# Three DRAM accumulators instead of four in a graph layer's scatter-add

## The chip, the cores and the metric

The kernel runs on one core of one Trainium2 chip. The metric is the device time of one execution in microseconds (us), as the median of several runs.

## The reference

One layer of a graph network with 6250 nodes, 200,000 edges and 128 features. Node rows are normalised and multiplied by a matrix; each edge makes a filter from its 20 attributes, multiplies it into the row of its `dst` node, and the products are added up at its `src` node; two small layers and a residual follow. Cut to what matters:

```python
h = jnp.maximum(_layernorm(x), 0.0)
xw = h @ W_in
W_ij = (shifted_softplus(f_ij @ W_f1 + b_f1) @ W_f2 + b_f2) * f_ij_cutoff
x_ij = xw[dst] * W_ij
out = jax.ops.segment_sum(x_ij, src, num_segments=6250)
return x + shifted_softplus(out @ W_o1 + b_o1) @ W_o2 + b_o2
```

`dst` is sorted and `src` is random, so reading node rows is local and adding the products up is not.

## The kernel before

**Quads.** 512 edges make a quad; there are 391 of them, in four chunks of 128 edges each (the last has fewer). The main loop runs over quads as a software pipeline: in iteration i, stage 1 of quad i (the filter's first layer: `s1_pe`, `s1_exp`, `s1_ln`), stage 2 of quad i-1 (filter and node rows on PE, `s2_copy` on ACT, and `s2_m`, the product, on DVE), then stage 3 of older quads. Everything else hangs in the iterations as hooks, under points such as "L" (loads), "D0", "PE2" or "S", which `run(i, point)` calls in a fixed order. So the order on each engine is written out by hand.

**Three ways to sum.** 168 quads are *sorted*: their rows are permuted by one-hot products and added up on PE into `accT`, a tile in SBUF that holds the sum with features on the partitions; what does not fit goes out in one overflow scatter for two quads (84 in all). The other 223 quads are *plain*: each chunk's 128 rows are added into DRAM by `scatter` (line 594), an indirect accumulating DMA issued by GpSimd (POOL). Of the plain quads 31 combine rows with equal `src` within the chunk first; 192 are *listed*, in 12 windows of 16: repeated rows go to list rows behind the accumulator, and at a window's end `l_load` reads these rows of every accumulator, `l_sum` adds them up by one matrix product per accumulator, and one further scatter adds the result. In all there are 768 + 123 + 96 = 987 scatters.

**Accumulators in DRAM.** There are `NACC` copies `accs[k]` (6272 node rows, 128 rows for rejects, and the list rows). `acc_of` deals the scatters out by their number n; two that add to the same copy may not overlap, so a scatter waits until the last one on its copy has landed. Before:

```python
        if k < K2_END:
            return k % 2
        if k < K3_END:
            return k % 3
        if k < RET:
            return k % 4
        return 1 + k % 3
```

`K2_END` is 8, `K3_END` 140, and `RET` is the number of scatters less 64, that is 923. The copies come into use one after the other because each must be filled with zeros first: `zero_piece` writes a copy's node rows in ten transfers, copies 0 and 1 from GpSimd's queue, copies 2 and 3 from SyncE's (SP) in the iterations of `Z2` and `Z3`; `zero_list` writes the list rows in three transfers.

**Retiring a copy.** After scatter 923 nothing is added to copy 0. From a few iterations later its rows are read in 13 groups of up to 512 nodes (`r0_load`, SP), transposed on PE (`r0_tp`) and added into `accT` on DVE (`r0_add`, line 1097), one group per iteration that has room.

**Output stage.** After the loop comes a check whose `For_i` blocks redo the work where an edge fell outside the fixed windows (on these inputs they run zero times). The output stage then loads three copies per group (`t_load`), adds them (`t_sum1` on GpSimd, `t_sum2` on GpSimd and DVE in turn), transposes, adds `accT`, and applies the two layers and the residual. Loads run five groups ahead (`TAIL_AHEAD`).

**Queues.** SP issues nearly all loads in program order, POOL issues the scatters in program order. DVE writes the product rows `s` of a listed quad, which the scatter reads, into a ring of four buffers.

Of the kernel before, what the change touches and what calls it, by code (L numbers as in the profile page):

```python
# [7 lines left out]
F32 = mybir.dt.float32  # L8
# [5 lines left out]
ALU = mybir.AluOpType  # L14
# [6 lines left out]
P = 128  # L21
# [22 lines left out]
WSEG = 256  # L44
HB = 64
NR = 3 * WIN
NACC = 4
FPARTS = ((0, 3), (3, 2), (5, 1))
CQ = 16
EARLY_N = 256  # L50
# [4 lines left out]
def tile_gnn(ctx: ExitStack, tc: tile.TileContext, x, fB, cT, srcT, srcr, dstr, win_, wf1, wf2, bias, bo1c, wo1,  # L55
             wo2, consts, ident, cmap, out, n_edges):
    nc = tc.nc
# [9 lines left out]
    spread = big(NSC)  # L67
    NCH = -(-n_edges // P)
    NQ = -(-NCH // 4)
    NPT = NP // P  # L70
    groups = node_groups(NP)
    tgroups = [(g * 512, min(4, (NP - g * 512) // P)) for g in range(-(-NP // 512))]
# [3 lines left out]
    GN = NP // GRP  # L76
    ZR = 10 if ACC_R % 10 == 0 else 1
    ZL = 3
    K1_END, K2_END, K3_END = 2, 8, 140
    Z2, Z3 = [0,0,1,1,2,2,3,3,4,4], [5+2*j for j in range(10)]  # L80
    mpq = sorted_quads(NQ)
    mpi = {q: n for n, q in enumerate(mpq)}
    units = unit_its(mpq)
    splain = [q for q in range(NQ) if q not in mpi]
    plain = {q: n for n, q in enumerate(splain)}
    NS = len(splain)
    LB, LE = listed(NS) if spread else (0, 0)
    CE = min(128, EP // P) if spread else EP // P
    CB = min(4 * NS + 64, EP // P) if spread else 0
    lend = splain[LE - 1] if LE else 0  # L90
    scat = [0] * (NQ + 60)
    for q in splain:
        scat[q + (2 if LB <= plain[q] < LE else 4)] += min(4, NCH - 4 * q)
    NW = (LE - LB) // SW
    LR = P * NW
    wend = [splain[LB + SW * (w + 1) - 1] for w in range(NW)]
    for w in range(NW):
        scat[wend[w] + 16] += 1
    for q in mpq[1::2] + mpq[-1:] * (len(mpq) % 2):
        scat[q + 10] += 1  # L100
    RET = max(120, sum(scat) - 64)
    ret_at = min(i for i in range(len(scat)) if sum(scat[:i + 1]) >= RET)

    cp = ctx.enter_context(tc.tile_pool(name="cp", bufs=1))
    dp = ctx.enter_context(tc.tile_pool(name="dp", bufs=1, space=DRAM))
# [1 line left out]
    ld = edge.enter_context(tc.tile_pool(name="ld", bufs=3))  # L107
    wk = edge.enter_context(tc.tile_pool(name="wk", bufs=2))
    sp_ = edge.enter_context(tc.tile_pool(name="sp", bufs=4))
    ps = edge.enter_context(tc.tile_pool(name="ps", bufs=2, space=PSUM))  # L110

    accs = []
# [15 lines left out]
    idt = cp.tile([P, P], F32, name="idt")  # L128
# [11 lines left out]
    accT = cp.tile([P, NP], F32, name="accT")  # L140
# [33 lines left out]

    def rows(t, o, T):
        n = min(T, 2)
        return t[o:o + T * P, :].rearrange("(h p t) f -> p h (t f)", p=P, t=n)

    def wide(t, T):
        return t.rearrange("p (h t) f -> p h (t f)", t=min(T, 2))  # L180

    def nodes(t, o, T):
        return t[:, o:o + T * P].rearrange("f (h p t) -> f h t p", p=P, t=min(T, 2))

    def tiles(t, T):
        return t[:, :T].rearrange("f (h t) p -> f h t p", t=min(T, 2))
# [5 lines left out]
    pst = {}  # L192
# [388 lines left out]
    def acc_of(k):  # L581
        if k < K1_END:
            return 0
        if k < K2_END:
            return k % 2
        if k < K3_END:
            return k % 3
        if k < RET:
            return k % 4
        return 1 + k % 3  # L590

    sc_n = [0]

# [256 lines left out]
    with tc.manual_schedule():  # L850
# [113 lines left out]
        def at(i, point, fn, *a):  # L964
            hooks.setdefault((i, point), []).append((fn, a))
# [6 lines left out]
        if CE < EP // P:  # L972
            w = (CE + 4 * NS) // 2
# [22 lines left out]
            at(2 * k + 3 if spread else 0, "D2", half_piece, k)  # L996
        for j in range(ZR):
            at(Z2[j] if spread else 0, "L", zero_piece, nc.sync, 2, j)
        for j in range(ZR):
            at(Z3[j] if spread else 0, "L", zero_piece, nc.sync, 3, j)  # L1000
        for g in range(1, NG):
            if not spread:
                xt_load(g)
# [74 lines left out]
        def large_all():  # L1078
            nc.vector.tensor_scalar(zcol[:, 3:4], late["lps"][:, 0:1], 0.0, None, op0=ALU.is_gt)

        def r0_load(g):
            o, T = tgroups[g]
            t_ = ld.tile([P, 4, P], F32, tag="fb", name="r0t", bufs=2)
            nc.sync.dma_start(wide(t_[:, :T], T), rows(accs[0], o, T))
            pst["r", g] = t_

        def r0_tp(g):
            T = tgroups[g][1]
            tp = ps.tile([P, 4, P], F32, tag="B", name="rtp", bufs=4)
            for t in range(T):  # L1090
                nc.tensor.transpose(tp[:, t, :], pst["r", g][:, t, :], idt)
            pst["p", g] = tp

        def r0_add(g):
            o, T = tgroups[g]
            v = nodes(accT, o, T)
            nc.vector.tensor_tensor(v, tiles(pst["p", g], T), v, op=ALU.add)

        def x_bias(t):
            n = min(4, NPT - t)  # L1100
            v = x_sb[:, t:t + n]
# [20 lines left out]
        for t in range(0, NPT, 4):  # L1122
            i = mid + 8 * (t // 4) if spread else 0
            at(min(i + 9, NQ + 1), "D2", x_bias, t)
        r0_at = 0
        for g in range(len(tgroups)):
            i = clear(max(r0_at + 1, ret_at + 5), units)
            r0_at = i
            at(i - 2, "L", r0_load, g)
            at(i, "PE2", r0_tp, g)  # L1130
            at(i + 1, "D0", r0_add, g)
        for r in range(-(-len(mpq) // RKQ)):
            i = mpq[RKQ * r]
            i = max(i, 6)
# [44 lines left out]
        if LE:  # L1179
            for k in range(NACC):  # L1180
                for j in range(ZL):
                    at((0, 3, 6, 9)[k] + j + 1, "L", zero_list, k, j)
        for q in mpq:
            at(q + 1, "D2", perm_oh, q)
            at(q + 2, "DR", part_rem, q, 1)
# [27 lines left out]
        for r in range(len(mpq) // RND):  # L1213
            for s, k in enumerate(unit_slots(mpq, r)):
# [2 lines left out]
                at(k, "PE2", unit_pe, r, s)  # L1217
                at(k + 1, "D1", unit_evac, r, s)

        banked = (prep_tp, prep_mm, rank_count, rank_over, permute, over_pe, over_row, over_sum, late_bias, r0_tp,  # L1220
                  l_count, l_sum, l_before, l_place)
        full = {-1: False}
        r0_end = r0_at
        s1_pe(0)
        for i in range(max(NQ + 7, last + 16, r0_end + 2, lend + 24)):
            if i % 2 == 0 and i // 2 + 2 <= (NQ - 1) // 2:
                load_sc(i // 2 + 2)
            run(i, "L")
            run(i, "D0")
            if i < NQ:  # L1230
                s1_oh(i)
            run(i, "D1")
            if 0 <= i - 1 < NQ:
                s1_eq(i - 1)
            if 0 <= i - 1 < NQ:
                s2_pe_x(i - 1)
                s2_pe_w(i - 1)
            if i + 1 < NQ:
                s1_pe(i + 1)
            if i < NQ:  # L1240
                s1_exp(i)
                s1_ln(i)
            if 0 <= i - 3 < NQ and not full[i - 1]:
                s3_copy(i - 3, 0)
                s3_copy(i - 3, 1)
            run(i, "A0")
            if 0 <= i - 4 < NQ:
                s3_ji(i - 4)
            run(i, "A1")
            if 0 <= i - 1 < NQ:  # L1250
                s2_copy(i - 1)
            run(i, "DM")
            if 0 <= i - 1 < NQ:
                s2_m(i - 1)
            if 0 <= i - 3 < NQ:
                s3_idx(i - 3)
            run(i, "DR")
            run(i, "PE1")
            full[i] = sum(fn in banked for fn, _ in hooks.get((i, "PE2"), [])) > 2
            if 0 <= i - 2 < NQ:  # L1260
                s3_pe(i - 2)
                if full[i]:
                    s3_copy(i - 2, 0)
                    s3_copy(i - 2, 1)
            run(i, "PE2")
            run(i, "A2")
            run(i, "D2")
            if 0 <= i - 4 < NQ and plainq(i - 4):
                s3_scatter(i - 4)
            if 0 <= i - 2 < NQ and i - 2 not in mpi and not plainq(i - 2):  # L1270
                s3_scatter(i - 2)
            run(i, "S")
# [20 lines left out]
    with tc.For_i(0, redo, 1):  # L1293
        anew = nc.values_load(flagi[:, 1:2], min_val=0, max_val=1, skip_runtime_bounds_check_because="0 or 1")
        with tc.For_i(0, anew, 1):
            nc.vector.memset(accT, 0.0)
            for k in range(1, NACC):
                for j in range(ZR):
                    zero_piece(nc.sync, k, j)
        trips = nc.values_load(flagi[:, 0:1], min_val=0, max_val=NCH,  # L1300
# [70 lines left out]
    with tc.manual_schedule():  # L1371
# [8 lines left out]

        def t_sum1(g):
            T = tgroups[g][1]
            a2 = tl[g][2]
            nc.gpsimd.tensor_tensor(a2[:, :T], a2[:, :T], tl[g][3][:, :T], op=ALU.add)

        def t_sum2(g):
            T = tgroups[g][1]
            a1 = tl[g][1]
            eng = nc.vector if g % 2 else nc.gpsimd
            eng.tensor_tensor(a1[:, :T], a1[:, :T], tl[g][2][:, :T], op=ALU.add)  # L1390

        def t_tp(g):
            tp = pt.tile([P, 4, P], F32, tag="tp", name="tp")
            for t in range(tgroups[g][1]):
                nc.tensor.transpose(tp[:, t, :], tl[g][1][:, t, :], idt)
            tl[g]["tp"] = tp

        def t_cp(g):
# [52 lines left out]
            del tl[g]  # L1451

        for g in range(min(TAIL_AHEAD, TG)):
            for k in (1, 2, 3):
                t_load(g, k)
        for j in range(-1, TG + 4):
            if TAIL_AHEAD <= j + TAIL_AHEAD < TG:
                for k in (1, 2, 3):
                    t_load(j + TAIL_AHEAD, k)
            if j + 1 < TG:  # L1460
                t_sum1(j + 1)
                t_sum2(j + 1)
            if 0 <= j < TG:
                t_tp(j)
            if 0 <= j - 1 < TG:
                t_cp(j - 1)
                t_z(j - 1)
            if 0 <= j - 3 < TG:
                t_act(j - 3)
                t_y(j - 3)  # L1470
            if 0 <= j - 1 < TG:
                t_ln(j - 1)
            if 0 <= j - 4 < TG:
                t_out(j - 4)
# [32 lines left out]
def clear(i, busy, n=1):  # L1507
    while any(i + k in busy for k in range(n)):
        i += 1
    return i  # L1510
# [113 lines left out]
```

## Time and profile before

| what | value |
|---|---|
| runs, median (lowest to highest) | 2063.21 us (2060.39 to 2073.85) |
| profiled execution, time / span | 2063.64 us / 2061.9 us |
| PE, DVE, ACT, POOL busy | 1820.4, 1650.9, 1470.8, 1652.4 us |
| scatters on POOL | 987, first at 57.8 us, last at 2007.3 us |
| output stage | about 2009 us to the end of the span |
| DMA | 272.41 MB, mean 132 GB/s |
| mean granted clock of PE | 0.952 |

Busy time is the time in which an engine executes; register, branch and DMA-issuing instructions of SP are not counted. A scatter counts as busy on POOL while its descriptors are made, not until its rows have landed. "Idle before, releaser" is the time in which an engine stood still ahead of an instruction, and what ended that; "issue" means that nothing that the profile shows was waited for. A row `line engine op out<-in xcount` groups like instructions, with their minimum, median and maximum time in ns in a view of one line. PE is TensorE, DVE VectorE, ACT ScalarE.

### The profile page before, as it was taken

What the parts mean: (1) busy time and instruction counts of PE and PEld (TensorE: products, weight loads), DVE (VectorE), ACT (ScalarE), POOL (GpSimd) and SP (SyncE); (2) the same over time, 40 slices, a digit from 0 to 9 for tenths busy, and PEclk for the clock granted to TensorE, in tenths of its full rate; (3) what the DMA queues carried; (4) which work ended last, traced back from release to release, by engine and by line L of the source; (5) the groups of instructions that cost most, each with busy time, mean ns of one, the idle gap of its engine ahead of it and who ended that gap; (6) DMA issues with size and microseconds to landing.
All of it is one profiled execution on the core that took longest, in us unless ns stands there. A gap on an engine that the chain in (4) does not pass through costs nothing.

```text
span 2061.9 us, 54889 instructions
## 1 busy us (share of the span) xinstructions
PE 1820.4 (88%) x19121; PEld 1188.1 (58%) x19121; DVE 1650.9 (80%) x4449; ACT 1470.8 (71%) x3999; POOL 1652.4 (80%) x1040
## 2 busy tenths in 40 slices
PE   2578998899999999899989999999799899999966
PEld 1455555556655665565656566566565556666734
DVE  3577897798987988888888989888788687787745
ACT  2458776777777787777778787787677677788714
POOL 3578887888888888878788888888888888888884
PEclk9789999999999999999999999999999999999987
DMA  6887766667676776667666666766666666667647
GB/s 240 242 202 141 129 123 123 111 111 144 118 136 120 128 136 111 130 115 131 129 121 125 121 126 117 126 117 132 113 116 114 125 105 118 108 119 141 128 44 250
DMA packets 359675, 272.41 MB, mean 132 GB/s; under 512 B 97727, under 2 KB 319850, under 8 KB 359394
## 3 DMA queue, kind: packets, MB, share of 16 engines
q0 software_dynamic: 143728, 71.30, 34.4%
q1 hardware_dynamic: 215378, 197.50, 32.8%
q8 instruction: 151, 2.47, 0.5%
q14 instruction: 130, 1.06, 0.2%
q10 hardware_dynamic: 288, 0.07, 0.0%
HBM read 154.45 MB, written 114.24 MB: 130 GB/s over the span
## 4 chain that ended last, share of the span: by engine, by line
PE 46%; DVE 20%; ACT 10%; DMA 7%; issue 6%; POOL 5%; SPq 4%; DVEq 0%; ACTq 0%; POOLq 0%
PE pq L702 15%; PE W L520 10%; PE un L795 8%; POOL acc L597 5%; ACT xc L525 3%; PE po L715 2%; DVE accT L806 2%; DVE pt L691 2%; PE z L328 2%; ACT mst L708 2%; DVE eql L384 2%; PE xg L512 2%; DMA acc<-s,lji 2%; DVE pm L677 2%; ACT a L333 2%
## 5 line engine op out<-in xcount | busy, mean ns | idle before, releaser
L597 POOL DMA_INDIRECT acc<-s,lji x768 | 1254.4, 1633 | 250.4 <-issue 185.5
L702 PE MATMUL pq<-pt,pm 128*128 128x387 bf16 x2688 | 545.6, 346 | 43.2 <-ACT pt L697 10.6
L525 ACT ACTIVATE xc<-xg,cb 128x128 f32<-128x128 f32 x1564 | 448.0, 377 | 80.5 <-PE xg L512 73.4
L520 PE MATMUL W<-w,a 128*128 128x128 f32 x3128 | 467.7, 294 | 0.0
L520 PEld LDWEIGHTS W<-w,a 128*128 128x128 f32 x3128 | 392.2, 197 | 42.9 <-issue 4.5
L708 ACT CAST mst<-pq 128x387 bf16<-128x387 f32 x672 | 305.4, 481 | 149.7 <-PE pq L702 108.7
L702 PEld LDWEIGHTS <-pm 128*128 128x128 bf16 x2688 | 261.1, 100 | 235.6 <-issue 60.9
L795 PE MATMUL un<-so,mst 32*128 32x392 bf16 x8064 | 372.5, 327 | 11.9 <-ACT s L555 5.8
L795 PEld LDWEIGHTS <-mst 32*128 32x128 bf16 x8064 | 226.1, 93 | 152.0 <-issue 45.3
L338 ACT ACTIVATE a<-a,con 128x512 f32<-128x512 f32 x391 | 282.3, 722 | 12.7
L597 POOL DMA_INDIRECT acc<-s,ji x123 | 198.4, 1613 | 80.1 <-issue 26.7
L333 ACT ACTIVATE a<-z 128x512 f32<-128x512 f32 x391 | 238.0, 609 | 30.5 <-PE z L328 20.1
L691 DVE TENSOR_TENSOR pt<-pt 128x512 f32<-128x512 f32 x336 | 231.6, 689 | 5.8
L535 DVE TENSOR_TENSOR pt<-W,xc 128x512 f32<-128x512 f32 x168 | 115.5, 687 | 132.4 <-PE po L715 62.9
L677 DVE TENSOR_SCALAR pm<-iot,pos 128x576 bf16<-128x576 f16 x672 | 219.8, 388 | 0.0
L535 DVE TENSOR_TENSOR s<-W,xc 128x512 f32<-128x512 f32 x192 | 131.8, 686 | 75.7 <-ACT xc L525 44.6
L780 DVE TENSOR_SCALAR so<-iot,mst 128x392 bf16<-128x392 f16 x672 | 181.2, 333 | 9.7 <-PE un L795 9.2
L597 POOL DMA_INDIRECT acc<-os,oji x96 | 158.1, 1647 | 30.4 <-issue 18.3
L806 DVE TENSOR_TENSOR accT<-un,accT 128x392 f32<-128x392 f32 x320 | 158.4, 557 | 28.6 <-PE un L795 18.9
L512 PE MATMUL xg<-wn,oh 63*128 63x128 bf16 x1564 | 158.9, 224 | 25.0 <-DVE oh L345 13.8
L328 PE MATMUL z<-ft,ws 123*128 123x512 bf16 x391 | 151.7, 388 | 15.5 <-POOL b2rep L942 9.3
L509 PE MATMUL W<-b2rep,onesb 64*128 64x512 bf16 x391 | 155.6, 398 | 0.2 <-issue 0.2
(210 smaller groups left out, 1968.1 us busy)
## 6 DMA issues: line engine op xcount, KB each, us to landing
rb<-reld SPq DMA_DIRECT2D x391, 64.0 KB
fsd<-f SPq DMA_DIRECT2D x49, 480.0 KB
ft<-fsd SPq DMA_DIRECT2D x195, 120.0 KB
sb<-src SPq DMA_DIRECT2D x169, 128.0 KB
fb<-in_fB_dram SPq DMA_DIRECT2D x49, 320.0 KB
ft<-fsd SPq DMA_DIRECT2D x195, 80.0 KB
wn<-tab SPq DMA_DIRECT2D x782, 15.8 KB
acc<-s,lji POOLq DMA_INDIRECT x768
```

Source lines behind the costliest of these rows:

```text
L333: nc.scalar.activation(a, st[q]["z"], AF.Exp)
L338: nc.scalar.activation(a, a, AF.Ln, bias=half, scale=0.5)
L512: nc.tensor.matmul(xg[:, c, :], st[q]["oh"][a:a + NR, c * P:(c + 1) * P], wn[a:a + NR, c // 2, :], start=True, stop=True)
L520: nc.tensor.matmul(W[:, c, :], st[q]["a"][:, c * P:(c + 1) * P], w2, start=False, stop=(c == 3))
L525: nc.scalar.mul(xc[:, c, :], st[q]["xg"][:, c, :], late["c", q // CQ][:, 4 * (q % CQ) + c:4 * (q % CQ) + c + 1])
L535: nc.vector.tensor_tensor(m[:, :, :P], st[q]["W"], st[q]["xc"], op=ALU.mult)
L597: nc.gpsimd.indirect_dma_start(out=accs[k][:rows, :], out_offset=bass.IndirectOffsetOnAxis(ap=ji, axis=0), in_=s, in_offset=None, compute_ ...
L677: nc.vector.tensor_scalar(pm[:, c], iot[:, :SLOTS], rk[r]["pos"][:, 4 * j + c:4 * j + c + 1], None, op0=ALU.is_equal)
L691: nc.vector.tensor_tensor(pt[:, :, k * P:(k + 1) * P], a, high(a), op=ALU.subtract)
L702: nc.tensor.matmul(t[:, :PW], mp[q]["pm"][:, c, s * P:(s + 1) * P], high(mp[q]["pt"][:, c:c + 1, :PW])[:, 0], start=(c == 0), stop=(c == 3))
L708: nc.scalar.copy(mp[q]["ms", s][:, :PW], mp[q].pop(("q", s))[:, :PW])
L795: nc.tensor.matmul(ts[g][:, :GN], mp[q]["ms", s][v, k * P:(k + 1) * P], mp[q]["oh"][v], start=(q == qs[0] and k == 0), stop=(q == qs[-1] a ...
```

## The change

There are three copies in DRAM. From scatter 8 on they take turns by three up to the end. The fourth copy's fills are gone (ten transfers and three list transfers), each window reads and adds three lists instead of four, copy 0 is no longer read and added into `accT` on the way, and the output stage reads copies 0, 1 and 2 instead of 1, 2 and 3.

```diff
-NACC = 4
+NACC = 3
...
-    K1_END, K2_END, K3_END = 2, 8, 140
-    Z2, Z3 = [0,0,1,1,2,2,3,3,4,4], [5+2*j for j in range(10)]
+    K1_END, K2_END = 2, 8
+    Z2 = [0, 0, 1, 1, 2, 2, 3, 3, 4, 4]
...
         if k < K2_END:
             return k % 2
-        if k < K3_END:
-            return k % 3
-        if k < RET:
-            return k % 4
-        return 1 + k % 3
+        return k % 3
...
-        for j in range(ZR):
-            at(Z3[j] if spread else 0, "L", zero_piece, nc.sync, 3, j)
...
-        def r0_load(g):
-            o, T = tgroups[g]
-            t_ = ld.tile([P, 4, P], F32, tag="fb", name="r0t", bufs=2)
-            nc.sync.dma_start(wide(t_[:, :T], T), rows(accs[0], o, T))
-            pst["r", g] = t_
-
-        def r0_tp(g):
-            T = tgroups[g][1]
-            tp = ps.tile([P, 4, P], F32, tag="B", name="rtp", bufs=4)
-            for t in range(T):
-                nc.tensor.transpose(tp[:, t, :], pst["r", g][:, t, :], idt)
-            pst["p", g] = tp
-
-        def r0_add(g):
-            o, T = tgroups[g]
-            v = nodes(accT, o, T)
-            nc.vector.tensor_tensor(v, tiles(pst["p", g], T), v, op=ALU.add)
...
-        r0_at = 0
-        for g in range(len(tgroups)):
-            i = clear(max(r0_at + 1, ret_at + 5), units)
-            r0_at = i
-            at(i - 2, "L", r0_load, g)
-            at(i, "PE2", r0_tp, g)
-            at(i + 1, "D0", r0_add, g)
...
-                    at((0, 3, 6, 9)[k] + j + 1, "L", zero_list, k, j)
+                    at((0, 3, 6)[k] + j + 1, "L", zero_list, k, j)
...
-            for k in range(1, NACC):
+            for k in range(NACC):
                 for j in range(ZR):
                     zero_piece(nc.sync, k, j)
...
         for g in range(min(TAIL_AHEAD, TG)):
-            for k in (1, 2, 3):
+            for k in range(NACC):
                 t_load(g, k)
```

In the output stage `t_sum1`, `t_sum2` and `t_tp` use the tiles of copies 0, 1 and 2 accordingly. The reckoning of `RET` (`scat`, `ret_at`) is removed, as is `r0_tp` from the list of functions that use PSUM's "B" banks, by which the loop decides where the evacuations of a combined quad stand on ACT.

More of the change, by code (lines that the diff above doesn't have):

```diff
@@ L90, in tile_gnn @@
     lend = splain[LE - 1] if LE else 0
-    scat = [0] * (NQ + 60)
-    for q in splain:
-        scat[q + (2 if LB <= plain[q] < LE else 4)] += min(4, NCH - 4 * q)
     NW = (LE - LB) // SW
@@ L96, in tile_gnn @@
     wend = [splain[LB + SW * (w + 1) - 1] for w in range(NW)]
[L97 to L102, printed above, removed]
     cp = ctx.enter_context(tc.tile_pool(name="cp", bufs=1))
@@ L1218, in tile_gnn @@
                 at(k + 1, "D1", unit_evac, r, s)
-        banked = (prep_tp, prep_mm, rank_count, rank_over, permute, over_pe, over_row, over_sum, late_bias, r0_tp,
+        banked = (prep_tp, prep_mm, rank_count, rank_over, permute, over_pe, over_row, over_sum, late_bias,
                   l_count, l_sum, l_before, l_place)
         full = {-1: False}
-        r0_end = r0_at
         s1_pe(0)
-        for i in range(max(NQ + 7, last + 16, r0_end + 2, lend + 24)):
+        for i in range(max(NQ + 7, last + 16, lend + 24)):
             if i % 2 == 0 and i // 2 + 2 <= (NQ - 1) // 2:
@@ L1382, in t_sum1 @@
             T = tgroups[g][1]
-            a2 = tl[g][2]
-            nc.gpsimd.tensor_tensor(a2[:, :T], a2[:, :T], tl[g][3][:, :T], op=ALU.add)
+            a1 = tl[g][1]
+            nc.gpsimd.tensor_tensor(a1[:, :T], a1[:, :T], tl[g][2][:, :T], op=ALU.add)
         def t_sum2(g):
             T = tgroups[g][1]
-            a1 = tl[g][1]
+            a0 = tl[g][0]
             eng = nc.vector if g % 2 else nc.gpsimd
-            eng.tensor_tensor(a1[:, :T], a1[:, :T], tl[g][2][:, :T], op=ALU.add)
+            eng.tensor_tensor(a0[:, :T], a0[:, :T], tl[g][1][:, :T], op=ALU.add)
         def t_tp(g):
@@ L1394, in t_tp @@
             for t in range(tgroups[g][1]):
-                nc.tensor.transpose(tp[:, t, :], tl[g][1][:, t, :], idt)
+                nc.tensor.transpose(tp[:, t, :], tl[g][0][:, t, :], idt)
             tl[g]["tp"] = tp
@@ L1457, in tile_gnn @@
             if TAIL_AHEAD <= j + TAIL_AHEAD < TG:
-                for k in (1, 2, 3):
+                for k in range(NACC):
                     t_load(j + TAIL_AHEAD, k)
```

## The prediction

> **What bounds the kernel now.** I read the page first (busy times, costliest groups), then busy time by stage, then what GpSimd waited for in each stage, and last the timeline around single scatters.
>
> ```profile
> span 2061.9 us, 54889 instructions
> PE 1820.4 (88%) x19121; PEld 1188.1 (58%) x19121; DVE 1650.9 (80%) x4449; ACT 1470.8 (71%) x3999; POOL 1652.4 (80%) x1040
> PE 46%; DVE 20%; ACT 10%; DMA 7%; issue 6%; POOL 5%; SPq 4%; DVEq 0%; ACTq 0%; POOLq 0%
> L597 POOL DMA_INDIRECT acc<-s,lji x768 | 1254.4, 1633 | 250.4 <-issue 185.5
> ```
>
> By these rows PE is the busiest and fills most of the chain that ended last, while POOL, 80% busy, has 5% of it. But a POOL instruction is always followed by a gap, and the gap is no spare time. From the stage 1090 to 1887 us:
>
> ```profile
>   issue: 98.2, 322
>   DMA acc<-s,lji: 6.7, 22
> ```
>
> 322 gaps in which nothing was waited for make 98.2 us, 0.305 us each; the 22 put down to a landing are the same length (6.7 by 22), so no landing delayed anything there. With 0.305 us for each scatter added to POOL's busy time, the stages read differently:
>
> ```profile
> core 0: us, PE busy (x) PEld busy (x) DVE busy (x) ACT busy (x) POOL busy (x), PEclk, DMA share, GB/s
> 173.00:357.00 184.00, 165.02 (x1675) 105.29 (x1676) 147.71 (x411) 133.08 (x367) 150.30 (x92) 0.94 0.67 125
> 357.00:840.00 483.00, 448.63 (x4882) 289.29 (x4880) 418.77 (x1163) 369.06 (x1014) 406.05 (x250) 0.98 0.68 125
> 840.00:1090.00 250.00, 226.71 (x2426) 145.72 (x2424) 212.58 (x605) 182.38 (x501) 202.67 (x124) 0.97 0.66 122
> 1090.00:1400.00 310.00, 296.40 (x3281) 191.48 (x3280) 272.60 (x733) 244.00 (x661) 261.48 (x160) 0.98 0.68 124
> 1400.00:1700.00 300.00, 270.64 (x2954) 172.94 (x2955) 243.08 (x647) 219.65 (x593) 253.32 (x154) 0.96 0.65 117
> 1700.00:1887.30 187.30, 181.04 (x1952) 118.87 (x1948) 146.93 (x376) 147.91 (x408) 157.16 (x99) 0.98 0.67 117
> 1887.30:2009.00 121.70, 101.30 (x1156) 71.15 (x1144) 76.70 (x198) 64.60 (x190) 100.27 (x64) 0.93 0.60 98
> ```
>
> Length less busy time less 0.305 per scatter leaves, stage by stage: 5.6 us (184 - 150.30 - 28.06), 0.7, 9.5, -0.3, -0.3, -0.1 and 1.9. So from 1090 us to the last scatter POOL issues scatters back to back, and a microsecond lost there is a microsecond of the total. Only 840 to 1090 us has spare time, and there POOL waited for products:
>
> ```profile
>   DVE s L535: 11.2, 5
> ```
>
> The bound of the second half is POOL's queue of scatter-adds (a wait inside it delays all that follow); in 840 to 1090 us it is the feed (PE, DVE, ACT).
>
> **Which scatters use three accumulators already.**
>
> ```profile
> 0.00:357.00 357.00, 229.87 (x140) 0.89 0.73 171
> 0.00:1887.30 1887.30, 1510.56 (x923) 0.96 0.68 131
> ```
>
> The rotation goes to four at scatter 140 (K3_END) and back to three at 923, which is RET for 987 scatters. By these counts that is 357 us and 1887 us. Before each scatter POOL waits until the last one on the same accumulator has landed: the third before it in rotation by three, the fourth in rotation by four. So the trace holds both rotations, and the 5.6 us and 1.9 us above are those on three.
>
> **The added wait.** The timeline at the end shows what it looks like (start, length, idle before it, releaser):
>
> ```profile
> 1902.58 1.54 POOL L597 DMA_INDIRECT acc<-os,oji  x1 [0.30 <-DMA acc<-s,ji]
> 1904.42 1.54 POOL L597 DMA_INDIRECT acc<-s,ji  x1 [0.31 <-ACT s L555]
> 1906.27 1.54 POOL L597 DMA_INDIRECT acc<-s,ji  x1 [0.30 <-issue]
> 1909.35 1.54 POOL L597 DMA_INDIRECT acc<-s,ji  x1 [1.54 <-DMA acc<-os,oji]
> ```
>
> Starts lie 1.85 us apart. The scatter of 1909.35 waits for that of 1902.58, the third before it. On time it would have started three slots (5.54 us) after it; the landing came too late for that, and the gap was 1.54 us instead of 0.30 (1.24 lost). In rotation by four the same landing has 7.4 us from the start and costs nothing. The change moves 923 - 140 = 783 scatters from four to three: 374 (250 + 124) before 1090 us and 409 (923 - 514, the sum of the counts so far being 140 + 374) after it.
>
> The mean stall per scatter in rotation by three is bounded by the two stages: 5.6 / 92 = 0.061 us from 173 to 357 us, and about 0.027 at the end (of the 1.9 us, 0.2 lie behind the last scatter: 1.7 / 64). Below them zero, if landings in the middle stay within three slots. By DMA share (0.65 to 0.68 in the middle, 0.67 early, 0.60 late) the early row is nearer; but it still holds the start's backlog, the last fill is issued inside it, and in part its idle time follows other waits (DVE, ACT), while the late row also has the retiring loads beside it. I take 0.025, the late row's side, and keep 0 and 0.061 for the range.
>
> At 0.025: 374 x 0.025 = 9.4 us before 1090 us, which the 9.5 us of spare time there hides; if that cover were gone they would cost their full 9.4. After it 409 x 0.025 = 10.2 us with nothing to hide them. Behind a waiting scatter stand all later scatters, and the rows that free their buffers late:
>
> ```profile
> ACT oji L769 <- DMA acc<-os,oji: 35.5, 6, 11.8
> ACT s L555 <- DMA acc<-s,ji: 19.0, 6, 8.4
> DVE s L535 <- DMA acc<-s,lji: 6.9, 5, 2.6
> ```
>
> ACT and DVE already wait for landings (four buffers of s, two of oji), and PE waits for them; SyncE's lm loads wait for the same landings. That is a second way to feel the stall, not a second cost: it moves the feed by what POOL is late.
>
> **What is removed at the start.** Ten fills and three list fills of the fourth accumulator:
>
> ```profile
> 50.00:100.00 50.00, 30.47 (x205) 25.15 (x205) 31.22 (x79) 24.03 (x68) 25.76 (x16) 0.73 0.85 237
> 100.00:150.00 50.00, 35.24 (x246) 24.06 (x247) 36.97 (x91) 28.96 (x83) 36.66 (x21) 0.80 0.85 215
> acc<-accT SPq DMA_DIRECT2D x20, 320.0 KB
> acc<-accT SPq DMA_DIRECT2D x12, 256.0 KB
> 79.68 0.48 SPq L168 DMA_DIRECT2D acc<-accT  x1
> 173.40 0.42 SPq L168 DMA_DIRECT2D acc<-accT  x1
>   DMA acc<-s,ji: 22.7, 16
> ```
>
> The two timeline rows are the first and last fill of that accumulator. Half of the 20 and three of the 12 are 4.06 MB (10 x 0.328 + 3 x 0.262). At 237 GB/s that is 17 us of traffic, some fifth of what moves in 80 to 173 us. The last row is POOL's wait for landings up to 173 us: 22.7 - 16 x 0.305 = 17.8 us of stalls, in rotations by one, two and three, beside that traffic. A fifth of them, about 4 us, may go; bounds are nothing and the 17 us. Whether an earlier POOL makes the feed of 840 to 1090 us earlier depends on how far the feed was held by POOL's buffers; I count half: -2 us. The removed issues, 13 at about 0.45 us, also free SyncE for ft and sb loads; that is inside the same 2 us.
>
> The Trainium skill ("DMA: Bandwidth & Descriptors", section "Issuing engines are not separate DMA queues") says that DMAs started from any engine run on the same 16 DMA engines and interleave. By that rule the fills do slow the scatters and -2 is the right sign; no row here separates the two.
>
> **What is removed on the way and at the end.**
>
> ```profile
> L484 PE MATMUL lsum<-lm,leq x96: 272/275/582, 347.6 to 1879.4; 128*128 128x128 f32 x96
> L1091 PE MATMUL rtp<-idt,r0t x49: 270/273/329, 1903.6 to 1997.8; 128*128 128x128 f32 x49
> L1097 DVE TENSOR_TENSOR accT<-rtp,accT x13: 292/678/692, 1905.9 to 1998.8; 128x512 f32<-128x512 f32 x12, 128x128 f32<-128x128 f32 x1
> SPq L1084 <- PE osum L755: 22.0, 4, 17.0
> r0t<-acc SPq DMA_DIRECT2D x12, 256.0 KB
> ```
>
> In each of 12 windows one of four lsum products goes (24 of 96 records, 24 x 0.275 = 6.6 us of PE) and one of four lm loads. At the end 49 transposes (13.4 us of PE), 13 additions (8.6 us of DVE) and 13 loads go, and SyncE no longer waits at them. All of that lies beside POOL's back-to-back queue (above, 0 to 2 us spare from 1090 us on), so its value is what it takes off the stalls: the loads are 3.2 MB of the 11.9 MB (98 GB/s x 121.7 us) moved in the last stage, a quarter of 1.7 us: -0.5 us, between 0 and -1.7. Without POOL as the bound the PE part would be worth up to 20 us.
>
> **What stays.** The output stage reads three accumulators either way, 39 loads, two additions per group. The order of instructions differs otherwise only in two evacuations on ACT that change places. The fill inside the skipped redo block runs no time.
>
> **Sum.** The profiled execution took 2063.64 us (span 2061.9 and 1.7 around it), the median of the runs is 2063.21. 2063.6 + 10.2 - 2 - 0.5 = 2071.3, so 2071 us.
>
> **Rivals.** One measurement of this kernel tells about 1% (20.6 us) from no change.
>
> *B, slower: the early stage's stalls all along.* At 0.061 per scatter, 374 x 0.061 = 22.8 us fall before 1090 us, 4 are saved at the start, 9.5 hidden: 9.3; then 409 x 0.061 = 24.9; less 0.5: 2063.6 + 33.7 = 2097. It decides from 0.044 on (783 x 0.044 - 4 - 9.5 - 0.5 = 20.5). For it: the same DMA share. Against: the late stage, with other traffic still running, stayed at 0.027.
>
> *C, no stalls.* The usual landing is soon:
>
> ```profile
> 2007.27 3.23 DMA acc<-os,oji
> ```
>
> 3.23 us from issue to landing, against 5.54 in three slots. If the middle lands like this, d = 0 and the time is 2063.6 - 2 - 0.5 = 2061. Against it: the 1.54 us gap above. The Trainium skill ("DMA: Bandwidth & Descriptors", section "Anatomy of one DMA") puts a DMA from GpSimd at some 2.0 us plus its bytes at 436 GB/s; for the 64 KB of a scatter that is an estimate of 2.15 us, and C follows from that rule. The trace differs in single cases: the scatter of 1902.58 took until about 1909.05 (0.30 before the start it held up), 6.5 us from its issue.
>
> *D, faster by over 1%.* The first 173 us are limited by bytes: all 17 us of the fills are gained and the feed follows, no stalls (C), -1.7 at the end: 2045. Over 1% it goes only if the PE work removed also counts, which POOL's full stages speak against.
>
> **Chances.** Forecast 0.60, B 0.20, C 0.16, D 0.04 (of which 0.03 past 1%). The forecast, C and 0.01 of D are within 1%: 0.77; slower 0.20; faster 0.03. Range 2055 (C with all of the 4 us and a little of D) to 2097 (B); the forecast's own 2062 to 2084.
>
> **What would show it.** Right: 987 scatters on three accumulators; in 357 to 1887 us gaps of over 0.31 us released by landings, adding up to 15 to 25 us; the stage with DVE waits smaller; the last scatter some 8 us later while the output stage keeps its 53 us; fewer stalls before 173 us. Wrong: no such gaps (C), gaps of over 35 us (B), POOL with spare time after 1090 us (then the feed is the bound and PE's savings count), or scatter landings that themselves grow.

## The result and the profile after

The changed kernel takes 2081.99 us (median of 15 runs, 2071.06 to 2095.77), the kernel before 2062.23 us beside it (15 runs). The ratio is 1.0097, with a 95% interval of 1.0079 to 1.0114: slower by 16 to 24 us. The forecast was 2071: the right sign, and less than half of the size. The measured time lies near the upper end of the forecast's own 2062 to 2084. The profiled execution took 2079.76 us, 16.1 us more than that of before (which lay 1.4 us above its median, this one 2.2 below).

The head of the page of the changed kernel:

```profile
span 2078.0 us, 54651 instructions
PE 1812.6 (87%) x19048; PEld 1178.5 (57%) x19048; DVE 1640.0 (79%) x4436; ACT 1468.1 (71%) x3999; POOL 1661.3 (80%) x1040
L584 POOL DMA_INDIRECT acc<-s,lji x768 | 1264.7, 1647 | 258.9 <-issue 187.1
```

PE and DVE have less work (7.8 and 10.9 us), as the diff says, and the span is longer. Busy time by stage, cut where the order of the scatters is the same as before (scatter 140, 514, 923, the last), first of before, then of the changed kernel:

```profile
core 0: us, PE busy (x) PEld busy (x) DVE busy (x) ACT busy (x) POOL busy (x), PEclk, DMA share, GB/s
357.00:1092.50 735.50, 677.84 (x7322) 437.15 (x7320) 633.01 (x1772) 553.17 (x1519) 610.81 (x374) 0.97 0.67 124
1092.50:1887.20 794.70, 745.49 (x8161) 481.07 (x8162) 660.85 (x1748) 609.82 (x1655) 669.87 (x409) 0.97 0.67 120
1887.20:2009.30 122.10, 101.40 (x1156) 71.23 (x1148) 76.80 (x198) 64.60 (x190) 100.27 (x64) 0.93 0.60 98
```

```profile
0.00:349.30 349.30, 254.88 (x2338) 172.17 (x2339) 254.07 (x699) 219.64 (x603) 248.98 (x173) 0.92 0.73 165
349.30:1095.30 746.00, 683.16 (x7356) 438.73 (x7358) 633.57 (x1773) 557.12 (x1531) 615.38 (x374) 0.97 0.66 121
1095.30:1903.80 808.50, 746.03 (x8101) 478.39 (x8097) 656.06 (x1739) 602.29 (x1638) 670.76 (x409) 0.97 0.66 117
1903.80:2025.90 122.10, 96.57 (x1099) 66.02 (x1091) 68.51 (x183) 63.87 (x190) 102.24 (x64) 0.89 0.53 71
```

The 16.1 us arise as follows. Scatter 140 comes at 349.3 us instead of 357.0: 7.7 us gained. The first half (374 scatters) is 10.5 us longer, the second (409) 13.8, the last stage the same, and the rest after it 0.5 shorter (52.1 for 52.6). -7.7 + 10.5 + 13.8 - 0.5 = 16.1. Length less POOL's busy time less 0.305 us per scatter, the idle time of POOL beyond its gaps, was 10.6 us in the first half, 0.1 in the second and 2.3 in the last stage; now it is 16.6, 13.0 and 0.3. The first half of the changed kernel, cut at 840 us as in the prediction:

```profile
349.40:840.00 490.60, 449.27 (x4873) 288.42 (x4872) 417.94 (x1159) 368.35 (x1013) 404.90 (x247) 0.97 0.67 123
840.00:1090.00 250.00, 228.49 (x2437) 147.04 (x2434) 212.07 (x606) 183.70 (x506) 205.99 (x126) 0.96 0.65 119
```

Here the idle time beyond the gaps is 10.4 and 5.6 us, where before had 0.7 and 9.5.

What POOL waited for from scatter 140 to 922 in the changed kernel, and between 840 and 1090 us (the last two rows):

```profile
  issue: 182.5, 597
  DMA acc<-s,lji: 32.6, 55
  DVE s L526: 3.2, 8
  issue: 29.4, 96
  DMA acc<-s,lji: 4.8, 7
```

55 waits for landings make 32.6 us, 15.8 beyond the usual gaps, where before such waits had only the length of the gap; more lies behind rows put down to another engine, so the sums by stage are the better measure. The waits for the product rows `s` in 840 to 1090 us (11.2 us by five before) are gone: POOL is now late enough to find these rows ready. One wait of 2.3 us for an overflow product is left there (`ACT os`).

The first 173 us, busy time before and after, and POOL's wait for landings after:

```profile
0.00:173.00 173.00, 97.03 (x649) 69.29 (x650) 104.01 (x280) 84.78 (x233) 96.91 (x81) 0.84 0.79 220
0.00:173.00 173.00, 98.92 (x682) 72.32 (x683) 108.88 (x289) 88.66 (x244) 101.76 (x84) 0.85 0.76 201
  DMA acc<-s,ji: 14.8, 9
```

With 19 GB/s less to move, the waits for landings fall from 22.7 us by 16 to 14.8 by 9.

### The profile page after: what moved, and what is told of

It reads as the page before. It is cut to its first block, busy times and chain, and to the rows that moved or that the text cites. A ratio compares the mean times of both kernels' runs of the same rounds, so it can differ in the third digit from the quotient of the medians.

```text
span 2078.0 us, 54651 instructions
## 1 busy us (share of the span) xinstructions
PE 1812.6 (87%) x19048; PEld 1178.5 (57%) x19048; DVE 1640.0 (79%) x4436; ACT 1468.1 (71%) x3999; POOL 1661.3 (80%) x1040
## 4 chain that ended last, share of the span: by engine, by line
PE 44%; DVE 19%; ACT 10%; DMA 8%; issue 7%; POOL 7%; SPq 3%; DVEq 0%; ACTq 0%; POOLq 0%
PE pq L689 15%; PE W L511 10%; PE un L782 8%; POOL acc L584 6%; ACT xc L516 3%; DMA acc<-s,lji 3%; DVE pt L678 3%; PE po L702 2%; DVE accT L793 2%; PE z L319 2%; DMA acc<-os,oji 2%; DMA acc<-s,ji 2%; ACT a L324 2%; ACT mst L695 2%; DVE eql L375 2%
## 6 DMA issues: line engine op xcount, KB each, us to landing
wn<-tab SPq DMA_DIRECT2D x782, 15.8 KB
```

## The experiments

Theory L: the loss is the wait for the third last landing; it counts in full where POOL issues back to back and is partly hidden where POOL waits for products. Rival U: it counts in full everywhere. Rival O: the rotation costs nothing, and the loss comes from the work that was removed or moved. The first four kernels share 17 runs of before (median 2058.53 us). The code shown is cut to what matters.

### Three in the middle, nothing else

```diff
         if k < RET:
-            return k % 4
+            return k % 3
         return 1 + k % 3
```

> The kernel before, with scatters 140 to 922 dealt out by three (copies 0, 1, 2) instead of four; copy 3 is filled, takes its turn in the last 64 scatters and is read as before, and copy 0 is retired as before. So only the wait changes. Theory L (a scatter waits for the landing of the third before it, and the loss counts where POOL issues back to back): 783 scatters at the 0.037 us that the changed kernel's stages show (28.7 us over 783) are 29 us, less the 9.5 us of spare time in 840 to 1090 us: 2062 + 19.5 = 2082 us. Rival U (POOL is the bound everywhere, nothing is absorbed): 2062 + 29 = 2091 us. Rival O (the rotation costs nothing, the loss comes from what was removed or moved: fills, retiring, list rows): 2062 us.

Measured: 2083.57 us, ratio 1.0121 (1.0095 to 1.0146), 20 to 30 us slower. O falls: the rotation alone costs as much as the whole change (16 to 24) or more. L and U both lie within the interval or at its edge (19.5 and 29). The second half of this run, in which POOL idles 19.1 us beyond its gaps:

```profile
1091.10:1908.40 817.30, 753.02 (x8215) 484.70 (x8211) 663.25 (x1755) 610.57 (x1653) 673.46 (x409) 0.97 0.67 117
```

### Three in the first half, three in the second

```diff
-    K1_END, K2_END, K3_END = 2, 8, 140
+    K1_END, K2_END, K3_END = 2, 8, 514
```

```diff
+        if k < 514:
+            return k % 4
         if k < RET:
-            return k % 4
+            return k % 3
```

> The kernel before, with scatters 140 to 513 by three and 514 to 922 by four (K3_END 514). L: 374 x 0.037 = 13.8 us of stalls, of which 9.5 lie in the spare time: 2066 us, and no wait of POOL for products between 840 and 1090 us. U: 2062 + 14 = 2076 us. O: 2062 us.

> The kernel before, with scatters 514 to 922 by three and 140 to 513 by four. L and U alike: 409 x 0.031 to 0.037 = 13 to 15 us, all of it on the path: 2075 to 2077 us. O: 2062 us. With the run of the first half on three it tells whether a stall costs the same wherever it falls (U: both near 2076) or only after 1090 us (L: 2066 and 2076).

Measured: 2064.78 us, ratio 1.0039 (1.0017 to 1.0060), so 8 us for the first half; 2081.42 us, ratio 1.0102 (1.0074 to 1.0130), 21 us for the second. By scatter that is 0.021 us in the first half (8 / 374) and 0.051 in the second (21 / 409). The second half on three alone costs as much as the whole change. For the first half L's 4 us lies in the interval (3.5 to 12.4 us), U's 14 and O's nothing do not. The second half costs more than the 13 to 15 us of both; its interval begins at 15. The rows of the second half on four (first) and on three (second):

```profile
1096.80:1888.90 792.10, 744.29 (x8134) 479.18 (x8138) 659.11 (x1745) 608.47 (x1646) 667.11 (x409) 0.97 0.69 120
1090.90:1902.90 812.00, 752.41 (x8202) 483.84 (x8202) 663.43 (x1753) 609.33 (x1651) 671.51 (x409) 0.97 0.67 118
```

Idle time of POOL beyond its gaps: 792.10 - 667.11 - 124.7 = 0.2 us on four, 812.00 - 671.51 - 124.7 = 15.7 on three, with POOL's own work 4.4 us apart. In the other kernels with four copies there it is 0.0 to 0.1 us (before, retiring left out, late fills).

### The fills put back

```diff
+    spare = dp.tile([ACC_R + LR, P], F32, name="spare")
+    fills = accs + [spare]
...
+        for j in range(ZR):
+            at(Z3[j] if spread else 0, "L", zero_piece, nc.sync, 3, j)
```

> The changed kernel, with the 13 fills of a fourth copy put back at their old places; they go to a tensor in DRAM that nothing reads. If the fills slow the scatters of the first 170 us and the gain from dropping them is kept to the end (POOL is without spare time in the changed kernel): the scatter 140 comes some 7.7 us later, as before, and the time is 2082 + 7 = 2089 us. If that gain is lost again on the way (POOL then waits for the feed): 2082 us.

Measured: 2086.79 us, ratio 1.0143 (1.0116 to 1.0170) against 1.0097 for the changed kernel without the fills: some 9 us, 3 to 16 by the two intervals together. Scatter 140 came at 361.1 us instead of 349.3:

```profile
0.00:361.10 361.10, 264.13 (x2327) 175.82 (x2328) 254.03 (x694) 220.03 (x600) 246.52 (x173) 0.88 0.75 170
```

So the fills do slow the start, and dropping them is worth more than the 2 us of the forecast. At least a part of the gain is kept to the end. How much is open: by scatter 514 the 11.8 us are down to 5.8 (1101.1 us instead of 1095.3), and that scatter comes anywhere from 1091.1 to 1101.1 us in the three kernels that have the fills and go by three in the first half.

### Retiring, and late fills

The next four share 23 runs of before (median 2066.96 us). The kernel before without the work of the retiring stage (it leaves out copy 0's share of the sum):

```diff
-            at(i - 2, "L", r0_load, g)
-            at(i, "PE2", r0_tp, g)
-            at(i + 1, "D0", r0_add, g)
```

> The kernel before without the retiring of copy 0: its 13 loads, 49 transposes and 13 additions are left out, and so copy 0's share of the sum. Rotation, fills and output stage are those of before. Theory L (POOL is the bound there): only the 1.7 us of stalls in the last 120 us can go: 2060 us where before has 2062. Rival (that work is on the path): 13.4 us of PE and 8.6 us of DVE less: 2042 to 2048 us.

Measured: 2066.82 us, ratio 0.9991 (0.9974 to 1.0007). Twenty-two microseconds of PE and DVE work removed are worth at most 5.4, as POOL's full stage said. The last stage of this run:

```profile
1892.90:2015.40 122.50, 96.53 (x1107) 66.27 (x1098) 68.95 (x185) 64.07 (x190) 101.22 (x64) 0.89 0.54 71
```

POOL still idles 1.8 us there (2.3 in before), though the retiring loads are gone and 71 GB/s move instead of 98.

The fourth copy's node rows filled later and used from scatter 450:

```diff
-    K1_END, K2_END, K3_END = 2, 8, 140
-    Z2, Z3 = [0,0,1,1,2,2,3,3,4,4], [5+2*j for j in range(10)]
+    K1_END, K2_END, K3_END = 2, 8, 450
+    Z2, Z3 = [0,0,1,1,2,2,3,3,4,4], [30+10*j for j in range(10)]
```

> The kernel before, with the ten fills of copy 3's node rows spread over iterations 30 to 120 (from a zero tile of their own) and its use begun at scatter 450 instead of 140 (K3_END 450); its list rows are filled early as before. The start loses 3.3 MB of its traffic, scatters 140 to 449 go by three, the second half by four. L: scatter 140 comes some 6 us earlier, 310 x 0.037 = 11.5 us of stalls follow, the spare time of 840 to 1090 us takes what is left over, and no stalls after: 2056 to 2062 us where before has 2062. U (every stall counts): 2062 - 6 + 11.5 = 2067 us.

Measured: 2068.19 us, ratio 1.0010 (0.9994 to 1.0027): no gain. The interval, 1 us faster to 6 slower, holds the upper end of L and also U. In its profile scatter 140 comes at 353.8 us instead of 357.0, and the first half is 10.0 us longer than in before (745.5 for 735.5): what the start wins, the first half takes back.

### What makes landings late

A landing is late when it holds up the third scatter after it: three slots leave some 3.7 us from a scatter's end (5.54 - 1.54 - 0.30). An sb load brings `src` numbers: it reads one row of 1 or 2 KB into all 128 partitions. From the trace's landing times: in the changed kernel, of the scatters 140 to 922 with an sb load issued beside them (from 3 us before their start to 1.5 us after their end) 21% landed over 3.6 us after their end, of the others 4%. So these loads were doubled, and as a control the same bytes were read without the broadcast:

```diff
             nc.sync.dma_start(t_[:, j * SEG:(j + n) * SEG],
                               src16[...].to_broadcast([P, n * SEG]))
+            nc.sync.dma_start(u_[:, j * SEG:(j + n) * SEG],
+                              src16[...].to_broadcast([P, n * SEG]))
```

> The changed kernel, with each sb load (one row of 1 or 2 KB read into all 128 partitions) issued a second time into a tile that nothing reads: 28 MB more traffic. In the trace of the changed kernel late landings cluster beside these loads. If these loads make them late, stalls of POOL after scatter 140 go from 29 us to 45 or more and the time from 2082 to 2095 to 2110 us. If the landings are late for other reasons: 2082 to 2086 us.

> The control: the same extra loads at the same places with the same bytes in each partition, but each partition reads its own bytes of the edge attributes. If only the bytes and packets on the 16 DMA engines count, the time and the stalls are those of the run with the doubled broadcast; if it is the broadcast of one row, the stalls stay near 29 us and the time within 5 us of 2082.

Measured: 2177.91 us with the broadcast (ratio 1.0536, 1.0497 to 1.0575), 2109.17 us with the same bytes spread (1.0209, 1.0180 to 1.0238). Against the changed kernel's 1.0097 that is some 90 and 23 us. Both miss what was expected: the control was to stay within 5 us and the broadcast to cost 13 to 28. So both count: the bytes alone make a quarter of the cost, and reading one row into 128 partitions the rest. Of the scatters 140 to 922 beside an sb load, by the same measure as above, 62% landed late with the broadcast doubled and 35% in the control; of the others 5 and 6%. The second half with the doubled broadcast, and with the control:

```profile
1154.60:1995.90 841.30, 756.47 (x8144) 485.17 (x8137) 659.12 (x1745) 603.23 (x1638) 669.15 (x409) 0.95 0.68 125
1113.80:1930.40 816.60, 746.71 (x8137) 480.15 (x8130) 658.64 (x1742) 603.49 (x1639) 671.83 (x409) 0.96 0.69 129
```

POOL's idle time there is 47.4 and 20.0 us, where the changed kernel has 13.0. The DMA share and GB/s of the two are alike, and so are packets and bytes (380,891 and 293.58 MB in both), so the mean load of the DMA engines does not tell how late a landing is.

The next three share 8 runs of before (median 2057.48 us). The doubled loads in the kernel before, on four:

> The kernel before with each sb load issued a second time into a tile that nothing reads. In rotation by four a landing has four slots, 7.4 us from the start of the scatter, 5.5 us after its end less the reaction, and with doubled loads in the changed kernel only 1 in 20 came later than some 5.3. If the 95 us that the doubled loads cost the changed kernel are waits of the rotation by three: here the first 140 scatters lose some 20 us (half of it absorbed in 840 to 1090 us), the last 64 some 8 and the middle under 8: 2080 to 2092 us. If the doubled loads delay the feed itself (ft, rb and sb come later): 2140 us or more.

Measured: 2111.89 us, ratio 1.0253 (1.0232 to 1.0274), 52 us and outside the 2080 to 2092 expected. By stages:

```profile
0.00:387.90 387.90, 273.10 (x2427) 182.37 (x2431) 258.59 (x706) 223.31 (x609) 244.66 (x173) 0.86 0.76 178
387.90:1136.30 748.40, 680.44 (x7224) 435.43 (x7217) 626.48 (x1757) 551.28 (x1508) 610.99 (x374) 0.96 0.73 135
1136.30:1936.40 800.10, 750.86 (x8187) 484.24 (x8189) 662.15 (x1750) 609.87 (x1655) 671.18 (x409) 0.97 0.72 132
```

The second half behaves as expected: 4.2 us of idle time on four against 47.4 on three, from the same loads, and 5.4 us more length than in before (800.1 for 794.7). Late landings are as many here (68% beside sb loads); with four copies they cost little. The miss is the start and what follows: scatter 140 comes 31 us later (the first scatters go by one, two and three copies), not 20, none of it is absorbed, and the first half takes 13 us more. What those 13 us wait for was not followed up; a slower feed is not excluded there.

The other way, 46 of the 49 fb loads (edge attributes) left out of the changed kernel (it then works with the first block's attributes):

> The changed kernel without 46 of the 49 loads of edge attributes (fb, 320 KB each, 15 MB in all); later blocks use the first block's attributes, so this part of the filter is left out. In the trace of the changed kernel 21% of the scatters beside these loads land over 3.6 us after their end, 6% of the others. If such loads are what makes landings late, some 30% of the late ones go: stalls after scatter 140 from 29 to about 20 us, 2073 us where the changed kernel has 2082. If a byte is a byte (15 of 264 MB): 2 us, 2080 us.

Measured: 2074.01 us, ratio 1.0079 (1.0040 to 1.0119). The interval holds both expectations, so this run settles nothing; the idle time of the second half is 10.9 us, for 13.0.

### Two in the middle

```diff
         if k < RET:
-            return k % 4
+            return k % 2
```

> The kernel before with scatters 140 to 922 dealt out by two. If the cost is the wait for the landing, two slots leave 1.9 us after a scatter's end, about the median landing: replayed with the landing times of before the 783 scatters stall 246 us, 0.31 each, and more where a second wait stands before the scatter: 2290 to 2400 us. If three is slow for another reason (the order of copies, list rows, what is loaded when): far less, under 2150 us.

Measured, in a single run: 2371.32 us, within what the wait for the landing gives.

```profile
361.50:1241.90 880.40, 714.90 (x7453) 455.78 (x7450) 636.40 (x1784) 563.53 (x1542) 612.09 (x374) 0.90 0.58 104
1241.90:2196.40 954.50, 783.43 (x8064) 496.69 (x8064) 655.40 (x1734) 603.79 (x1627) 667.65 (x409) 0.90 0.57 100
```

POOL idles 154 and 162 us beyond its gaps, 0.40 per scatter, about the whole difference to before (314 us; before idles 10.7 in both). In the second half, by copies in turn: 0.1 us (four), 13 to 19 (three, in the changed kernel and the three variants with ordinary loads), 162 (two).

## Why the prediction was right and wrong

**Right: the bound and the mechanism.** POOL's scatter queue bounds the second half: leaving out 22 us of PE and DVE work in the last stage gained at most 5.4 us, and three copies alone cost 25 us. (Of the 22, the 13 additions are 8.4 us by their row, not 8.6.) The gaps that the prediction asked for are there: from scatter 140 to 922, 33 gaps of over 0.31 us were released by landings, 17.9 us beyond the usual 0.305. The output stage kept its length. The last scatter, though, came 16.6 us later and not 8.

**Wrong by size: the stall per scatter.** The step that failed is "I take 0.025, the late row's side". In the second half the changed kernel idles 13.0 / 409 = 0.032 us, the runs with three copies beside it 0.033 to 0.047 (13.6 us with the fills back, 19.1 with three in the middle), and in time the second half on three costs 21 us (15 to 27), not 10.2. The late row was no chance value: in ten kernels with ordinary loads that stage, always on three, idles 0.3 to 3.7 us, 2.0 in the mean, as in before. But it is not the middle. Six sb loads stand beside its 64 scatters (0.09 each), 70 beside the 409 of the second half (0.17), 19 beside the 92 of the early row (0.21). Late landings stand beside these loads, so this would put the three rows in the order in which they were measured; that it is the whole reason is argued and not tested. The retiring loads, by which the prediction held the late row for rather too dear, did not matter: without them the stage idles 1.8 us. The early row, 0.061, erred the other way; it is above all idle times of the second half (three copies, ordinary loads), but not outside the interval of the time (0.037 to 0.066). The DMA share, by which the middle was nearer to the early row, pointed the right way; the doubled loads show that it is no measure of late landings (0.68 and 0.69 at 47.4 and 20.0 us).

**Wrong by size: "which the 9.5 us of spare time there hides".** The first half on three costs 8 us (3.5 to 12.4), not nothing. There is cover, but the stalls were more than it could hide: at 0.037 us, 374 scatters stall 13.8 us. In the profile of the changed kernel 10.4 us of idle time stand before 840 us instead of 0.7, and only 3.9 of them are taken back after it (5.6 instead of 9.5). The cover was also taken from one profile: the whole first half on four idles 10.6 us in before, but 8.1 and 6.0 in the two other kernels that have the same start (three in the second half, retiring left out). The half is 10.5 us longer, 6.0 of them idle time; the other 4.6 are longer scatters, and POOL's own time in that half differs as much between runs on four (609.5 to 617.4).

**Wrong by size, other sign: the fills.** Forecast -2; measured 7.7 us at scatter 140, and some 9 us (3 to 16) at the end when they were put back. "A fifth of them, about 4 us" was too small. Whether "I count half" was wrong is open: it had no row behind it, but by scatter 514 about half of the gain is gone in the profiles.

**The sum again.**

| term, us | forecast | profile, before to after | separate runs |
|---|---|---|---|
| fills dropped | -2 | -7.7 | -9 (-16 to -3) |
| first half on three | 0 | +10.5 | +8 (3.5 to 12.4) |
| second half on three | +10.2 | +13.8 | +21 (15 to 27) |
| retiring dropped, output stage | -0.5 | -0.5 | -2 (-5 to +1) |
| sum | +7.7 | +16.1 | +18 |

The whole change measured 20 (16 to 24). The intervals of the separate runs are wide, so that their sum comes near does not prove each term. Luck had a part: the fills gained 6 to 7 us more than forecast and so hid a part of what the two halves cost beyond it. Of the rivals, B priced the stall too high, and C and D fell: landings in the middle are not all like the quick one at the end. The 0.044 from which B was to decide lies between the stall by idle time (0.032 in the changed kernel) and by time (0.051).

**On the rules weighed.** That DMAs from all queues run on the same 16 engines and interleave (the Trainium skill, "DMA: Bandwidth & Descriptors", "Issuing engines are not separate DMA queues") agrees with the fills, some 9 us, though no run here tells the engines from the memory behind them. The fixed 2.0 us plus bytes at 436 GB/s for a DMA from GpSimd (the Trainium skill, "DMA: Bandwidth & Descriptors", "Anatomy of one DMA") would leave no stalls on three copies; the 13.0 us of the second half speak against it as a price for every landing.

## What to carry to other kernels

A wait on the n-th last transfer is paid by the late landings, not by the usual one: price it from stages with the same neighbours, and count how much room n slots leave (here four slots cost 0.1 us in 409 scatters, three 13, two 162). Add each engine's issue gaps to its busy time before deciding what bounds a stage: 80% busy was a full queue here. Spare time in one stage is used once, and a value of it from one profile is a rough one (in three kernels alike in their first half POOL idles 6.0 to 10.6 us there).

## What the runs showed of the hardware

A load that reads one row of 1 or 2 KB into all 128 partitions delays the scatter-adds beside it more than its bytes do. On three copies 29 MB more of it raised POOL's idle time in the second half from 13.0 to 47.4 us, the same bytes from distinct addresses to 20.0, at like DMA shares (0.68 and 0.69); the whole kernel took some 90 and 23 us longer. On four copies the same loads cost 52 us, of which the second half has 5.

The scatter-adds' own packets took no longer for it. Queue q0 (nearly all scatter-adds), in the changed kernel, with the broadcast doubled and in the control; then q1 (nearly all that SP issues) in the same order:

```profile
q0 software_dynamic: 143728, 71.30, 34.3%
q0 software_dynamic: 143728, 71.30, 32.5%
q0 software_dynamic: 143728, 71.30, 33.8%
q1 hardware_dynamic: 208370, 189.43, 31.5%
q1 hardware_dynamic: 236594, 218.67, 36.6%
q1 hardware_dynamic: 236594, 218.67, 36.2%
```

With the spans of 2078.0, 2177.6 and 2105.9 us the shares of q0 are 713, 708 and 712 us of all 16 engines, those of q1 655, 797 and 762. So the 28,224 added packets took 142 us as a broadcast and 107 as plain reads: they are a third slower themselves, while those of the scatter-adds are not. That leaves waiting ahead of their packets, or behind them, for what makes the scatter-adds late; the runs do not tell which. Why the broadcast is slower (one place in memory read 128 times, or something else) was not tried.
